# Reordering GpSimd's and SyncE's queues in a fused attention and mixture-of-experts kernel: the context's second sum, the result stores, the two real rows, and a third residual buffer

## The chip, the cores and the metric

The kernel runs on one core of a Trainium2 chip. The core has five engines, each with its own in-order instruction queue: TensorE (PE in the profile; its weight loads are PEld), VectorE (DVE), ScalarE (ACT), GpSimd (POOL) and SyncE (SP). SyncE and GpSimd issue the transfers of this kernel: SyncE plain ones, GpSimd those that add into their target and those with a list of rows ("indirect"). A queue that waits for a semaphore holds everything behind it.

The metric is the device time of one execution in microseconds (us). All data are 32-bit floats.

## What is computed

The reference is cut here to its steps:

```python
# attention, for 32 sequences of 512 tokens x 512 channels
q   = layernorm(x) * (1 + 0.1 * (s - 0.5)) * (1 + 0.1 * wave)   # s: ten logistic steps of sigmoid(|row|)
Q, K, V = q @ Wq.T + bq, mem @ Wk.T + bk, mem @ Wv.T + bv       # mem: the context times a constant
Qf, Kf, Vf = (fft(t, axis=sequence) for t in (Q, K, V))
QKV = hamilton(hamilton(Qf * filt, Kf * filt), Vf * filt)       # quaternion products of four channel blocks
x   = x + ifft(QKV).real
# mixture of experts over all 16384 tokens, 8 experts, a capacity for each
tokens = layernorm(x, gamma, beta)
logits = tokens @ gate_weight.T
top1, weight = argmax(logits), softmax(logits)[top1]            # weight is zero for tokens over the capacity
h   = gelu(dispatch @ wi[e]);  expert_out = h @ wo[e]           # 512 -> 2048 -> 512
out = x + weight * expert_out
```

A Fourier transform over 512 positions becomes matrix products with fixed tables. The spectrum of a real sequence is symmetric, so half of it is computed. Sums and differences of a sequence's front half and its mirrored rear half (the "folds") let the tables be half as large. Two lines of the spectrum are purely real (the first, and the middle one); they sit together in one partition and get a product of their own.

## The kernel before, in words

**Stages.** `attention_and_routing` handles the 32 sequences one after the other. I call each a *row*; b is its number. Then `experts` gathers the tokens of each expert, multiplies with its weights by a block scheme with fewer products (line 1226), and adds into the output by indirect stores (line 1378). A row's attention takes about one row period, but its work is spread over three: its context and x come in during the two rows before, and its normalisation, routing and stores happen in the rows behind.

**The order of the work** is written by hand. Every step is put into a heap with a due time, `at(time, function, ...)`, and `steps(...)` does it for a sequence of small ones. base[b] is the due time at which row b begins, 57.5 planner units after the row before. The heap is emptied in order of time, and `in_order` (line 158) then pins each engine's instructions to that order. So due times are only an order. What an engine really does when depends on the data.

**A row on TensorE**: the forward tables on the folded context (`ps_cf`, line 531) and on the folded query input (`ps_qf`, lines 539 and 544); then six projections k0, q0, v0, k1, q1, v1 (`pp_k`, `pp_q`, `pp_v`, line 576), which share two PSUM buffers in turn; between them the inverse tables of the row before (`back`, line 728), transposes and router logits of older rows. I give times inside a row from its first `ps_cf` matmul: "+25" is 25 us after it.

**The context's path.** `load_ctx` brings the direct half of the context by SP (line 454) and the mirrored half by two indirect loads of POOL (`behind`, line 273). POOL adds the halves (`add_ctx` 0, line 464), ScalarE negates the mirrored half (`minus_ctx`, line 459), and POOL adds the input once more from DRAM (`add_ctx` 1, line 464, `ctx<-in_ctx`), which gives the difference. VectorE folds both (`fold_ctx`, line 483, `cs<-ctx`) in the next row, ahead of the blocks of `pp_k` (line 595) that end the use of `pp_k`'s PSUM buffer.

**The two real lines' path** (`real_lanes`, from line 606). ScalarE copies them from the projections into a small tile `ny` (line 584) for k, q and v. SP stores it to DRAM (`nyid<-ny`, line 612) and loads it back spread over the partitions (`nyi<-nyid`, line 620). POOL multiplies in 15 small operations (lines 630 to 643). SP stores the product (`nyod<-nyo`, line 651) and puts it into `y` (`y<-nyod`, line 655), which the inverse tables (`back`) read.

**The residual's path.** ScalarE copies the sine part (`sines`, line 735), VectorE makes sum and difference (`part`, lines 742 and 745; `upper`, line 748), POOL adds the odd part (`lower`, line 755, `r<-y`) and then the input x (`add_input`: line 762 direct, line 273 twice indirect, `r<-in_x`). From r come the norms, the tokens (line 853), the result (line 861), and two stores (`store`, lines 865 to 872): the tokens by SP (`tokbuf<-tok`, line 869), and the result as a direct half by SP (`out<-r`, line 871) and two indirect stores by POOL (line 273, `out<-r,back`). The stores to `out` wait for one another, since all write the same tensor. The pool `resp` holds r in two buffers.

**POOL's queue in a row before**, from the middle of one row to the middle of the next: `r<-y`; `r<-in_x` and its two indirect parts; four scatters of routing entries (`meta<-entry,slot`, line 988); the product of the two real lines; the two indirect result stores; `ctx<-in_ctx` (the second sum); `qs<-x` and `x<-x` (line 496); the next context's indirect loads.

Due times that the change touches stand in one line each for the context (its fields are tx, tn, ta, tf, tl, cf, cl, cn, c0, c1) and for the real lines:

```python
}.get(b, (13.2, 17.4, 18.7, 31.0, 40.5, 16.3, 19.4, 44.4, 29.0, 53.0))
real_lanes(b, o + 35.1, *((o + 42.5, o + 48.3) if last else (o + 46.0, o + 58.5)))
at(o2 + 48.5, store, b, a["out"], "r")
```

Of the kernel before, what the change touches and what calls it, by code (L numbers as in the profile page):

```python
# [11 lines left out]
F32 = mybir.dt.float32  # L12
I32 = mybir.dt.int32
AF = mybir.ActivationFunctionType
ALU = mybir.AluOpType
# [203 lines left out]
def attention_and_routing(tc, a, gain, ident, gamma, beta, tokbuf, meta):  # L219
    nc = tc.nc  # L220
# [15 lines left out]
    with ExitStack() as es:  # L236
# [11 lines left out]
        yp = pool("yp", 1)  # L248
        resp = pool("resp", 2)
        tokp = pool("tokp", 1)  # L250
# [16 lines left out]

        def behind(b, ap, tiles, store=False, add=False):


            for h, t in enumerate(tiles):
                at_row = bass.IndirectOffsetOnAxis(ap=back[:, b, h : h + 1], axis=0)
                ins = nc.gpsimd.indirect_dma_start(
                    out=ap if store else t,
                    out_offset=at_row if store else None,
                    in_=t if store else ap,
                    in_offset=None if store else at_row,
                    bounds_check=n_tok - 1,
                    oob_is_err=False,
                    **({"compute_op": ALU.add} if add else {}),  # L280
                )
            return ins

# [167 lines left out]
        def load_ctx(b):  # L451

            w[b]["ctx"] = c = inp.tile([P, 2, H, D], F32, tag="ctx", name=f"ctx_{b}")
            nc.sync.dma_start(c[:, 0], onward(ctx_in[b]))
            behind(b, flat_rows(ctx_in), [c[:, 1, h] for h in range(H)])

# [103 lines left out]
        def project(b, n, c, t0, t1, t_blk):  # L560
# [20 lines left out]
            def real_rows():  # L581
                if "ny" not in w[b]:
                    w[b]["ny"] = nyp.tile([1, 3, 2, D], F32, tag="ny", name=f"ny_{b}", bufs=1)
                nc.scalar.copy(w[b]["ny"][:, i], w[b][key][0:1])

# [15 lines left out]
            if c == 0:  # L601
                at(done + 0.55, real_rows)
            at(t_blk, block, slice(0, 4, 3), ALU.subtract)
            at(t_blk + 0.6, block, slice(1, 3), ALU.add)

        def real_lanes(b, t, t_mul, t_out):

            def out():  # L610
                w[b]["nyid"] = dr.tile([6, D], F32, tag="nyid", name=f"nyid_{b}")
                nc.sync.dma_start(
                    w[b]["nyid"].rearrange("n d -> (n d)").unsqueeze(0),
                    w[b]["ny"].rearrange("o n l d -> o (n l d)"),
                )

            def back_in():
                w[b]["nyi"] = nyp.tile([P, 3, 2, 2, 2], F32, tag="nyi", name=f"nyi_{b}", bufs=1)
                with nc.allow_non_contiguous_dma(reason="two rows"):
                    nc.sync.dma_start(  # L620
                        w[b]["nyi"].rearrange("p n l h j -> p (n l) h j"),
                        w[b]["nyid"].rearrange("n (h f j) -> f n h j", h=2, j=2),
                    )
# [29 lines left out]
            def back():  # L653
                with nc.allow_non_contiguous_dma(reason="two rows"):
                    marks["row"] = nc.sync.dma_start(
                        w[b]["y"][0:1, 0].rearrange("o r (g f) -> o (r g) f", f=P),
                        w[b]["nyod"].rearrange("f x -> x f").unsqueeze(0),
                    )

            at(t, out)  # L660
            at(t + 3.8, back_in)
            steps(t_mul, 0.1, multiply())
# [94 lines left out]
        def add_input(b, way):  # L757
            r = w[b]["r"]
            if way:
                behind(b, flat_rows(x_in), [r[:, 2 * h + 1] for h in range(H)], add=True)  # L760
            else:
                nc.gpsimd.dma_start(r[:, 0::2, :], onward(x_in[b]), accum_op=ALU.add)
# [35 lines left out]
        def residual(b, t0, t1, t_in):  # L798

            for c, t in enumerate((t0, t1)):  # L800
                at(t, inverse, b, c)
                at(t + 1.85, sines, b, c)
                at(t + 2.5, part, b, c, 0)
                at(t + 3.1, part, b, c, 1)
            at(t1 + 3.7, upper, b)
            at(t1 + 4.6, lower, b)
            for way in range(2):
                at(t_in + 0.5 * way, add_input, b, way)
# [55 lines left out]

        def store(b, to, n):

            rows = to[b * S : (b + 1) * S, :]
            if n == "tok":
                marks[n, b] = nc.sync.dma_start(tok_rows(rows), w[b][n])
            else:  # L870
                nc.sync.dma_start(onward(rows), w[b][n][:, 0::2, :])
                marks[n, b] = behind(b, to, [w[b][n][:, 2 * h + 1] for h in range(H)], store=True)

# [186 lines left out]
        for b in range(B):  # L1060
# [5 lines left out]
                1: (27.8, 30.9, 32.0, 40.0, 50.0, 27.5, 30.5, 49.2, 40.0, 53.0),  # L1066
            }.get(b, (13.2, 17.4, 18.7, 31.0, 40.5, 16.3, 19.4, 44.4, 29.0, 53.0))
            if b + 1 < B:
# [28 lines left out]
            if b == 0:  # L1097
                real_lanes(b, o + 45.4, o + 53.0, o + 60.0)
                pt = 29.2, 51.2, 60.2, 38.2, 61.6, 71.0
            else:  # L1100
                real_lanes(b, o + 35.1, *((o + 42.5, o + 48.3) if last else (o + 46.0, o + 58.5)))
                if last:
                    pt = 30.6, 40.4, 49.2, 53.0, 62.4, 71.2
                else:
                    pt = 30.6, 41.6, 51.0, 54.4, 64.2, 73.6
# [15 lines left out]
            if b < B - 2:  # L1121
# [3 lines left out]
                steps(o2 + 12.5, 0.42, norms(b))  # L1125
                at(o2 + 30.0, store, b, tokbuf, "tok")
                at(o2 + 48.5, store, b, a["out"], "r")
                for dc, (t0, t1) in enumerate(((33.35, 35.5), (37.25, 38.3), (44.6, 45.2), (52.95, 53.6))):
                    at(o2 + t0, transposes, b, dc, range(TC))
                    at(o2 + t1, turned, b, dc)  # L1130
                lp, sh, lg, ch, cd, ct, rk, we, pl, sc = (
                    (66.25, 70.05, 73.15, 74.0, 0.5, 83.0, 85.65, 89.0, 90.0, 102.5)
                    if b < B - 3
# [11 lines left out]
            elif b == B - 2:  # L1145
                for t in range(TC):
                    at(end + 15.2 + 0.72 * t, token, b, t)
                    at(end + 34.0 + 0.72 * t, result, b, t)
                steps(end + 12.5, 0.17, norms(b))
                at(end + 17.9, store, b, tokbuf, "tok")  # L1150
                at(end + 37.0, store, b, a["out"], "r")
                for dc in range(DC):
# [12 lines left out]
            else:  # L1165
# [4 lines left out]
                for t in range(TC):  # L1170
                    at(end + 28.2 + 0.72 * t, token, b, t)
                    at(end + 40.7 + 0.72 * t, result, b, t)
                    for dc in range(DC):
                        at(end + 31.5 + 0.72 * t, transposes, b, dc, (t,), lambda dc=dc: two(dc))
                at(end + 31.1, store, b, tokbuf, "tok")
                at(end + 43.6, store, b, a["out"], "r")
                for dc in range(DC):
# [74 lines left out]
def experts(tc, a, ident, gamma, beta, tokbuf, meta, marks):  # L1252
# [9 lines left out]
    with ExitStack() as es:  # L1262
# [41 lines left out]

        with after(marks["row"]):
            wi = [load_wi(0, g) for g in range(G)]
        for g, t in enumerate(wi):
# [79 lines left out]

        with after(marks["r", B - 2]):
            wo = load_wo(0)
        xt = turn(0, 0, gather(0, 0))  # L1390
# [74 lines left out]
```

## Time and profile before

| what | value |
|---|---|
| median of 3 runs | 3630.23 us (3629.61 to 3639.62) |
| the profiled execution | 3633.5 us, its span 3631.8 us |
| mean granted TensorE clock | 0.983 |
| busy PE, DVE, ACT, POOL | 3484.9, 2465.1, 1513.3, 1197.4 us |
| row 0's first matmul to the last projection of row 31 | 13.6 to about 1939.9 us |
| from there to the first expert's first transpose (`ept`) | 1939.9 to 2027.5 us |
| experts, to the end of the span | 2036.5 to 3631.8 us |

The profile shows one execution. Busy times are sums of instruction lengths; they do not say which engine others waited for. That stands in the waits: "PE pp_v L576 <- DVE before L943" means that TensorE stood before a projection and that VectorE's instruction of line 943 was the last thing to end before it went on. The instruction named is the last in VectorE's order, so the true cause may lie some instructions earlier on VectorE. In a timeline each row is an instruction or a run of equal ones: its start from the span's start, its length, engine, line, what it writes and reads, and in brackets how long its engine sat idle before it and what ended that. "L464 POOL DMA_DIRECT2D" is the issue of a transfer by GpSimd; the transfer lands later.

### The profile page before, as it was taken

Reading aid. Unit: us, or ns where it says so; the run is one execution under the profiler, and the core shown is the slowest. Engines: PE = TensorE matmul, PEld = TensorE weight load, DVE = VectorE, ACT = ScalarE, POOL = GpSimd, SP = SyncE. Lnnn points to the kernel's source line nnn. Section 1 sums busy time; section 2 is a strip of 40 time slices with the busy share of each in tenths; the row PEclk is TensorE's granted clock in tenths of the full one; section 3 lists DMA queues with packets and bytes.
Section 4 is the critical chain, followed back from the end, with each engine's and each line's share of the span. In section 5 each row is a group of like instructions: output and inputs, shape, how many; then the busy total and the mean of one; then the engine's idle time right before and its main releaser. Section 6 shows DMA issues by size and latency. Waiting matters only on the chain. (4 is left out here: it accounts for less than half of the span.)

```text
span 3631.8 us, 39890 instructions
## 1 busy us (share of the span) xinstructions
PE 3484.9 (96%) x14080; PEld 2419.9 (67%) x14080; DVE 2465.1 (68%) x4430; ACT 1513.3 (42%) x2885; POOL 1197.4 (33%) x1166
## 2 busy tenths in 40 slices
PE   8899999999999999999996699999999999999998
PEld 4454555455555555555553588888888888888887
DVE  7998889798989898988887544353444444443532
ACT  5676677667555555555553211211212222211111
POOL 2344545455555454646553211110011111111100
PEclk9999999999999999999997899999999999999999
DMA  6767777676666667575736212130313121111200
GB/s 206 173 162 170 176 168 182 164 185 152 151 142 138 152 131 159 124 168 117 169 76 158 61 47 70 36 101 13 104 32 105 35 87 41 53 58 42 87 1 1
DMA packets 313064, 399.27 MB, mean 110 GB/s; under 512 B 115072, under 2 KB 181120, under 8 KB 312832
## 3 DMA queue, kind: packets, MB, share of 16 engines
q0 software_dynamic: 81040, 189.44, 26.0%
q1 hardware_dynamic: 230096, 207.01, 18.9%
q8 instruction: 111, 1.82, 0.2%
q14 instruction: 89, 0.73, 0.1%
q10 hardware_dynamic: 1728, 0.27, 0.0%
HBM read 239.37 MB, written 85.00 MB: 89 GB/s over the span
## 5 line engine op out<-in xcount | busy, mean ns | idle before, releaser
L1226 PE MATMUL r_o<-wo,h 128*128 128x256 f32 x3584 | 781.2, 379 | 0.0
L1226 PE MATMUL r<-xt,wi 128*128 128x256 f32 x3584 | 778.7, 380 | 0.8 <-DVE u L1241 0.8
L1226 PEld LDWEIGHTS r<-xt,wi 128*128 128x128 f32 x3584 | 682.2, 190 | 93.9 <-DVE u L1241 1.1
L1226 PEld LDWEIGHTS r_o<-wo,h 128*128 128x128 f32 x3584 | 677.5, 190 | 90.3
L576 PE MATMUL pp_v<-wv,cf 128*128 128x512 f32 x1024 | 472.5, 605 | 43.9 <-DVE before L943 37.6
L576 PE MATMUL pp_q<-wq,qf 128*128 128x512 f32 x1024 | 457.3, 595 | 0.9 <-DVE blk L595 0.9
L576 PE MATMUL pp_k<-wk,cf 128*128 128x512 f32 x1024 | 458.0, 595 | 0.0
L1378 POOL DMA_INDIRECT out<-o,ids x64 | 106.9, 1671 | 912.1 <-ACT o L1375 802.9
L576 PEld LDWEIGHTS pp_v<-wv,cf 128*128 128x128 f32 x1024 | 194.7, 194 | 288.6 <-issue 233.5
L1404 ACT ACTIVATE h<-h 128x512 f32<-128x512 f32 x256 | 160.0, 629 | 474.0 <-DVE h L1234 473.7
L576 PEld LDWEIGHTS pp_k<-wk,cf 128*128 128x128 f32 x1024 | 187.3, 190 | 225.2 <-issue 220.2
L576 PEld LDWEIGHTS pp_q<-wq,qf 128*128 128x128 f32 x1024 | 189.8, 190 | 217.4 <-issue 216.3
L1339 POOL DMA_INDIRECT g<-tokbuf,ids x64 | 80.6, 1259 | 509.9 <-PE ept L1357 491.7
L1375 ACT ACTIVATE o<-u_o,wgt 128x256 f32<-128x256 f32 x96 | 43.5, 500 | 385.4 <-DVE u_o L1234 385.4
L988 POOL DMA_INDIRECT meta<-entry,slot x128 | 175.0, 1367 | 57.7 <-issue 38.4
L1234 DVE TENSOR_TENSOR h<-r,u 128x512 f32<-128x512 f32 x192 | 129.6, 686 | 73.3 <-PE r L1226 73.1
L1241 DVE TENSOR_TENSOR u_o<-r_o,p_o 128x512 f32<-128x512 f32 x16 | 11.1, 691 | 239.7 <-PE r_o L1226 239.7
L892 ACT ACTIVATE tokT<-pt,beta,gamma 128x512 f32<-128x512 f32 x124 | 95.8, 774 | 156.1 <-PE pt L881 155.4
L699 DVE TENSOR_TENSOR pa<-pa,pb 128x1024 f32<-128x1024 f32 x128 | 157.4, 1230 | 2.9
L701 DVE TENSOR_TENSOR pa<-pa,pb 128x1024 f32<-128x1024 f32 x128 | 156.0, 1219 | 0.0
L696 DVE TENSOR_TENSOR pb<-blk 128x1024 f32<-128x1024 f32 x128 | 155.9, 1218 | 0.0
L696 DVE TENSOR_TENSOR pa<-blk 128x1024 f32<-128x1024 f32 x128 | 155.8, 1217 | 0.1
(212 smaller groups left out, 5376.6 us busy)
## 6 DMA issues: line engine op xcount, KB each, us to landing
xs<-in_x SPq DMA_DIRECT2D x32, 1024.0 KB, 6.8
x<-in_x SPq DMA_DIRECT2D x32, 1024.0 KB, 7.2
tokbuf<-tok SPq DMA_DIRECT2D x32, 1024.0 KB, 13.3
wi<-in_wi SPq DMA_DIRECT2D x64, 512.0 KB, 3.9
wo<-in_wo SPq DMA_DIRECT2D x32, 1024.0 KB, 5.1
qs<-x POOLq DMA_DIRECT2D x61, 512.0 KB, 5.1
ctx<-in_ctx SPq DMA_DIRECT2D x32, 512.0 KB, 3.8
r<-in_x POOLq DMA_DIRECT2D x32, 512.0 KB, 8.4
```

Of the source, the lines that this page charges most:

```text
L576: nc.tensor.matmul(w[b][key][:, ri, :], w[b][f][:, dc, lo : lo + P], wt[n][:, dc, :], start=(dc == 0), stop=(dc == DC - 1),)
L696: tt(out, _bc(left, full), right, ALU.mult)
L699: tt(pa[:, :, 0], pa[:, :, 0], pb[:, :, 1], ALU.subtract)
L701: tt(pa[:, :, 1], pa[:, :, 1], pb[:, :, 0], ALU.add)
L892: nc.scalar.activation(to, ps, AF.Identity, bias=o, scale=g)
L988: nc.gpsimd.indirect_dma_start(out=meta[t], out_offset=bass.IndirectOffsetOnAxis(ap=w[b]["slot"][:, t : t + 1], axis=0), in_=entry[:, b, t ...
L1226: nc.tensor.matmul(to[:, m, :], lhs(a, m, i), rhs(b, i), start=(i == 0), stop=(i == k - 1))
L1234: tt(c[i], x, y, ALU.add)
L1339: nc.gpsimd.indirect_dma_start(out=t, out_offset=None, in_=tokbuf, in_offset=bass.IndirectOffsetOnAxis(ap=gid[:, e, c : c + 1], axis=0), b ...
L1375: nc.scalar.activation(o[:, d * N : (d + 1) * N], c[2 * h + d][:, m, :], AF.Copy, scale=wgt[:, e, col : col + 1])
L1378: nc.gpsimd.indirect_dma_start(out=a["out"], out_offset=bass.IndirectOffsetOnAxis(ap=tid[:, e, col : col + 1], axis=0), in_=o, in_offset=None,
L1404: [lambda o=o: nc.scalar.activation(o, o, AF.Gelu) for o in out],
```

## The change

- **The context's second sum** is due at 44.5 rather than 53.0, and the negation ahead of it at 41.5 rather than 44.4 (rows 2 on; rows 0 and 1 keep theirs). On POOL it then stands behind `r<-in_x` and ahead of the product of the two real lines.
- **The product** stands ahead of the four scatters.
- **The result store** is split into `store_on` (SP, direct half) and `store_behind` for h = 0 and 1 (POOL, indirect). In rows up to 28 the order is: h = 0 ahead of `r<-in_x`, h = 1 after the scatters, and the direct half in the next row, behind `y<-nyod` on SP. The last three rows keep the direct half first.
- **nyid** is stored in three pieces of 4 KB, one after each of the copies for k, q and v, through a one-buffer tile of 4 KB; before it was one store of 12 KB after the last copy.
- **The odd part** (lines 745 and 748) is due 1.6 later; on VectorE one of the matrix product's operations (1.22 us) goes ahead of it.
- **`resp`** has three buffers. The buffer is 8 KB per partition; `ny` shrinks by as much.
- **Row 30's results** are due ahead of row 31's tokens on ScalarE.
- **Expert 0's weights**: three quarters of wi are loaded after row 30's `y<-nyod`, the last quarter and wo after row 31's; before, all of wi came after row 31's and wo after row 30's result store.

TensorE's order is unchanged. The diff's core:

```diff
-        resp = pool("resp", 2)
+        resp = pool("resp", 3)
...
             def real_rows():
-                if "ny" not in w[b]:
-                    w[b]["ny"] = nyp.tile([1, 3, 2, D], F32, tag="ny", name=f"ny_{b}", bufs=1)
-                nc.scalar.copy(w[b]["ny"][:, i], w[b][key][0:1])
+                w[b]["ny", n] = nyp.tile([1, 2, D], F32, tag="ny", name=f"ny_{n}_{b}", bufs=1)
+                nc.scalar.copy(w[b]["ny", n], w[b][key][0:1])
+
+            def real_rows_out():
+                if "nyid" not in w[b]:
+                    w[b]["nyid"] = dr.tile([3, 2 * D], F32, tag="nyid", name=f"nyid_{b}")
+                nc.sync.dma_start(w[b]["nyid"][i : i + 1], w[b]["ny", n].rearrange("o l d -> o (l d)"))
...
                 at(done + 0.55, real_rows)
+                at(done + 1.65, real_rows_out)
...
-            at(t, out)
-            at(t + 3.8, back_in)
+            at(t, back_in)
...
-                at(t + 2.5, part, b, c, 0)
-                at(t + 3.1, part, b, c, 1)
-            at(t1 + 3.7, upper, b)
-            at(t1 + 4.6, lower, b)
+                at(t + 2.5 + 1.6 * c, part, b, c, 0)
+                at(t + 3.1 + 1.6 * c, part, b, c, 1)
+            at(t1 + 5.3, upper, b)
+            at(t1 + 6.2, lower, b)
...
-            else:
-                nc.sync.dma_start(onward(rows), w[b][n][:, 0::2, :])
-                marks[n, b] = behind(b, to, [w[b][n][:, 2 * h + 1] for h in range(H)], store=True)
+        def store_on(b):
+            nc.sync.dma_start(onward(a["out"][b * S : (b + 1) * S, :]), w[b]["r"][:, 0::2, :])
+
+        def store_behind(b, h):
+            marks["r", b] = behind(b, a["out"], h, w[b]["r"][:, 2 * h + 1], store=True)
...
-            }.get(b, (13.2, 17.4, 18.7, 31.0, 40.5, 16.3, 19.4, 44.4, 29.0, 53.0))
+            }.get(b, (13.2, 17.4, 18.7, 31.0, 40.5, 16.3, 19.4, 41.5, 29.0, 44.5))
...
-                real_lanes(b, o + 35.1, *((o + 42.5, o + 48.3) if last else (o + 46.0, o + 58.5)))
+                real_lanes(b, o + 38.9, *((o + 39.5, o + 48.3) if last else (o + 45.0, o + 58.5)))
...
-                at(o2 + 48.5, store, b, a["out"], "r")
+                if b < B - 3:
+                    at(o2 + 40.2, store_behind, b, 0)
+                    at(o2 + 52.0, store_behind, b, 1)
+                    at(o2 + 65.0, store_on, b)
+                else:
+                    at(o2 + 42.9, store_on, b)
+                    at(o2 + 44.5, store_behind, b, 0)
+                    at(o2 + 51.0, store_behind, b, 1)
...
-                    (66.25, 70.05, 73.15, 74.0, 0.5, 83.0, 85.65, 89.0, 90.0, 102.5)
+                    (66.25, 70.05, 73.15, 74.0, 0.5, 83.0, 85.65, 89.0, 90.0, 104.5)
...
-                    at(end + 34.0 + 0.72 * t, result, b, t)
+                    at(end + 25.4 + 0.7 * t, result, b, t)
...
-                at(end + 37.0, store, b, a["out"], "r")
+                at(end + 28.3, store_on, b)
+                for h in range(H):
+                    at(end + 28.3 + (0.1, 1.7)[h], store_behind, b, h)
...
-        with after(marks["row"]):
-            wi = [load_wi(0, g) for g in range(G)]
+        with after(marks["row", B - 2]):
+            wi = [load_wi(0, g) for g in range(G - 1)]
+        with after(marks["row", B - 1]):
+            wi.append(load_wi(0, G - 1))
+            wo = load_wo(0)
...
-        with after(marks["r", B - 2]):
-            wo = load_wo(0)
```

More of the change, by code (lines that the diff above doesn't have):

```diff
@@ L266, in onward, with behind @@
             return ap.rearrange("(h w p) d -> w p h d", h=H, p=P)[0]
[L268 to L282, printed above, removed]
+        def behind(b, ap, h, t, store=False, add=False):
+            at_row = bass.IndirectOffsetOnAxis(ap=back[:, b, h : h + 1], axis=0)
+            return nc.gpsimd.indirect_dma_start(
+                out=ap if store else t,
+                out_offset=at_row if store else None,
+                in_=t if store else ap,
+                in_offset=None if store else at_row,
+                bounds_check=n_tok - 1,
+                oob_is_err=False,
+                **({"compute_op": ALU.add} if add else {}),
+            )
         w = [{} for _ in range(B)]
@@ L454, in load_ctx @@
             nc.sync.dma_start(c[:, 0], onward(ctx_in[b]))
-            behind(b, flat_rows(ctx_in), [c[:, 1, h] for h in range(H)])
+            for h in range(H):
+                behind(b, flat_rows(ctx_in), h, c[:, 1, h])
         def minus_ctx(b):
@@ L606, in real_lanes @@
         def real_lanes(b, t, t_mul, t_out):
[L610 to L615, printed above, removed]
             def back_in():
@@ L621, in back_in @@
                         w[b]["nyi"].rearrange("p n l h j -> p (n l) h j"),
-                        w[b]["nyid"].rearrange("n (h f j) -> f n h j", h=2, j=2),
+                        w[b]["nyid"].rearrange("n (l h f j) -> f (n l) h j", l=2, h=2, j=2),
                     )
@@ L654, in back @@
                 with nc.allow_non_contiguous_dma(reason="two rows"):
-                    marks["row"] = nc.sync.dma_start(
+                    marks["row", b] = nc.sync.dma_start(
                         w[b]["y"][0:1, 0].rearrange("o r (g f) -> o (r g) f", f=P),
@@ L759, in add_input @@
             if way:
-                behind(b, flat_rows(x_in), [r[:, 2 * h + 1] for h in range(H)], add=True)
+                for h in range(H):
+                    behind(b, flat_rows(x_in), h, r[:, 2 * h + 1], add=True)
             else:
@@ L863, in result, with store_tokens @@
             )
[L865 to L869, printed above, removed]
-            else:
-                nc.sync.dma_start(onward(rows), w[b][n][:, 0::2, :])
-                marks[n, b] = behind(b, to, [w[b][n][:, 2 * h + 1] for h in range(H)], store=True)
+        def store_tokens(b):
+            marks["tok", b] = nc.sync.dma_start(tok_rows(tokbuf[b * S : (b + 1) * S, :]), w[b]["tok"])
+        def store_on(b):
+            nc.sync.dma_start(onward(a["out"][b * S : (b + 1) * S, :]), w[b]["r"][:, 0::2, :])
+        def store_behind(b, h):
+            marks["r", b] = behind(b, a["out"], h, w[b]["r"][:, 2 * h + 1], store=True)
         def transposes(b, dc, ts, psum=None):
@@ L1097, in attention_and_routing @@
             if b == 0:
-                real_lanes(b, o + 45.4, o + 53.0, o + 60.0)
+                real_lanes(b, o + 49.0, o + 53.0, o + 60.0)
                 pt = 29.2, 51.2, 60.2, 38.2, 61.6, 71.0
             else:
-                real_lanes(b, o + 35.1, *((o + 42.5, o + 48.3) if last else (o + 46.0, o + 58.5)))
+                real_lanes(b, o + 38.9, *((o + 39.5, o + 48.3) if last else (o + 45.0, o + 58.5)))
                 if last:
@@ L1125, in attention_and_routing @@
                 steps(o2 + 12.5, 0.42, norms(b))
-                at(o2 + 30.0, store, b, tokbuf, "tok")
-                at(o2 + 48.5, store, b, a["out"], "r")
+                at(o2 + 30.0, store_tokens, b)
+                if b < B - 3:
[6 more added lines that the diff above has]
+                    at(o2 + 51.0, store_behind, b, 1)
                 for dc, (t0, t1) in enumerate(((33.35, 35.5), (37.25, 38.3), (44.6, 45.2), (52.95, 53.6))):
@@ L1147, in attention_and_routing @@
                     at(end + 15.2 + 0.72 * t, token, b, t)
-                    at(end + 34.0 + 0.72 * t, result, b, t)
+                    at(end + 25.4 + 0.7 * t, result, b, t)
                 steps(end + 12.5, 0.17, norms(b))
-                at(end + 17.9, store, b, tokbuf, "tok")
-                at(end + 37.0, store, b, a["out"], "r")
+                at(end + 17.9, store_tokens, b)
+                at(end + 28.3, store_on, b)
+                for h in range(H):
+                    at(end + 28.3 + (0.1, 1.7)[h], store_behind, b, h)
                 for dc in range(DC):
@@ L1174, in attention_and_routing @@
                         at(end + 31.5 + 0.72 * t, transposes, b, dc, (t,), lambda dc=dc: two(dc))
-                at(end + 31.1, store, b, tokbuf, "tok")
-                at(end + 43.6, store, b, a["out"], "r")
+                at(end + 31.1, store_tokens, b)
+                at(end + 43.6, store_on, b)
+                for h in range(H):
+                    at(end + 43.6 + (0.1, 1.7)[h], store_behind, b, h)
                 for dc in range(DC):
```

## The prediction

> **What bounds the kernel now.** I read the busy times first, then what TensorE waited for, then single rows in order of time. The profiled execution took 3633.5 us (span 3631.8); the runs' median is 3630.23, so its own time is 3.3 above the median. Busy times (us, share of the span, count):
> ```profile
> PE 3484.9 (96%) x14080; PEld 2419.9 (67%) x14080; DVE 2465.1 (68%) x4430; ACT 1513.3 (42%) x2885; POOL 1197.4 (33%) x1166
> ```
> TensorE's waits (total us, times, longest):
> ```profile
> PE pp_v L576 <- DVE before L943: 37.6, 17, 5.7
> ...
> PE lg L911 <- ACT tokT L905: 14.1, 3, 12.2
> ...
> PE back L728 <- DMA y<-nyod: 10.5, 2, 6.7
> ```
> TensorE is the bound, so a change that leaves its work alone can only win its gaps. The page's 96% hides two places. The experts' 1595 us (from 2036.5) are matmul without gaps and stay. In the 32 rows of attention, row 3 starts at 197.5 and row 31 at 1881.5: 1684 us for 28 rows. Rows without a gap take 58.27 (the start of row 15 to that of row 16 is 58.3), 28 of them 1631.6; the excess is **52.4 us**, 40 of it in rows 3 to 14. (It is more than the waits' sum because after a wait of 4.6 us or more the next four to eight matmuls come every 0.86 us instead of 0.43.) Two rows by windows (columns: length, then busy us of PE, PEld, DVE, ACT, POOL, granted clock, DMA share, GB/s):
> ```profile
> 379.70:445.40 65.70, 60.02 (x209) 32.40 (x208) 52.83 (x92) 43.34 (x92) 36.16 (x37) 0.97 0.78 192
> 937.00:995.30 58.30, 58.30 (x210) 31.86 (x209) 53.49 (x99) 32.59 (x58) 29.68 (x29) 1.00 0.65 145
> ```
> What the slow row waited for stands in its timeline (start, length, engine, line, operation; in brackets the idle time before it and its releaser):
> ```profile
> 394.27 1.81 POOL L273 DMA_INDIRECT out<-r,back  x1 [0.16 <-issue]
> 399.34 0.98 POOL L273 DMA_INDIRECT out<-r,back  x1 [3.27 <-ACT qs L491]
> 400.32 1.37 POOL L464 DMA_DIRECT2D ctx<-in_ctx  x1
> 406.46 1.23 DVE L483 TENSOR_TENSOR cs<-ctx 128x1024 f32<-128x1024 f32 x1 [8.03 <-PE back L728]
> 410.50 0.68 DVE L595 TENSOR_TENSOR blk<-pp_k,xz_k 128x512 f32<-128x512 f32 x1
> 412.03 1.19 PE L576 MATMUL pp_v<-wv,cf 128*128 128x512 f32 x1 [5.68 <-DVE before L943]
> ```
> POOL issues the context's second sum behind the real rows' products and both strided stores. It lands about 6 us later; VectorE, whose order is fixed, stands 8.03 us before the fold that reads it, and the blocks that free pp_k's PSUM buffer stand behind the fold. The releasers printed are the last ones by the profile (back had long been done); the transfer is the true one. Over all rows the fold's idle time is 90.5 us:
> ```profile
> L483 DVE TENSOR_TENSOR cs<-ctx 128x1024 f32<-128x1024 f32 x62 | 75.6, 1221 | 90.5 <-issue 44.9 <-DMA ctx<-in_ctx 23.0 <-PE back L728 15.8
> ```
> Row by row the landing after the row's start (first number) gives the row's length (second): 4: 25.3, 65.7; 5: 19.7, 58.2; 6: 26.6, 65.7; 7: 22.4, 60.0; 11: 25.9, 65.6; 13: 21.9, 59.6; 14: 25.9, 64.9; 15: 19.0, 58.3. The fold is ready for its data at +17.7 to +18; some 2 us of lateness are free.
>
> The second place is the end of row 31:
> ```profile
> 1940.08 0.69 SPq L655 DMA_DIRECT2D y<-nyod  x1
> 1946.61 3.75 PE L728 MATMUL back<-y,inv 128*128 128x512 f32 x4 [6.71 <-DMA y<-nyod]
> 1953.75 0.97 POOL L273 DMA_INDIRECT out<-r,back  x1 [6.14 <-issue]
> 1959.71 0.59 ACT L735 COPY r<-back 128x512 f32<-128x512 f32 x1 [19.15 <-DMA out<-r,back]
> 1960.33 1.29 DVE L742 TENSOR_TENSOR r<-back,r 128x512 f32<-128x512 f32 x2 [13.05 <-ACT r L735]
> ```
> ScalarE waits 19.15 us for the buffer of row 29's result, VectorE 13.05 behind it, and the chain goes on serially to the first expert's matmul at 2027.5.
>
> **The change part by part.** *Context's sum (due 53.0 to 44.5), negation (44.4 to 41.5).* On POOL it now goes right behind the three issues of r<-in_x, which are done at +50 to +56 of the row before (they wait for r<-y, landing +49 to +51 in rows 3 to 14, +43 to +45 later). Issue 1.4, landing 5.9: it is there by about +4 of its row, 14 us ahead of the fold. The negation it needs ends at +45 to +53 today and moves earlier. Rows with landing under 20 show what remains: nothing. Upper bound: all 52.4. Lower: half the early rows' 40.2 and all of the later rows' 12.2, 32. I take **45**, nearest to rows 5 and 15, leaving 7 for waits with other causes (VectorE is busy 52.8 to 53.5 of 58.3, so small lateness stays).
>
> *What is queued behind it.* The multiply (15 small operations, 8.5 to 10.6 us) starts 1.4 later by the sum but ahead of four scatters (1.367 each, 5.5) and the stores: it ends at about +6 of the next row; nyod and y<-nyod (6.3 to 9.3 to landing) are in by +18, needed by back at +24.7. Free. The scatters are read only after row 31. qs<-x waits for ScalarE at +19.9 as now: free, if the second strided store leaves by then. It is issued at +8 to +15.5 and no longer waits 3.27 for the first one's landing, which lies 15 us back.
>
> *Result stores in three.* Same bytes. The direct half, last in the write order, waits on SP for the second strided half: +13 to +20 (landing 4.1 after issue). Behind it on SP stand nyid for k, the context's load and the following xs. The context's load left at +25.7 (471.35 in the row of 445.4), so it has 5 us.
>
> *nyid in three 4 KB stores, one 4 KB buffer.* SP issues 64 more DMAs of 0.25 to 0.4 us, on an idle queue. ScalarE's copy for q (at +25.5) must now find k's store landed: issued at +18.7 (copy at +17.6, 1.0 long) to +20.8, landing 1.4 (nyod, 4 KB) to 7 later (nyid's 12 KB to nyi's issue in busy rows; 1.5 to 3 in quiet ones). So +20.1 to +27.8: 0 to 2.3 us of ScalarE's time in busy rows, where pp_q's buffer is needed only some 5 us later. I take 0; at 2.3 in rows 3 to 14 and no cover it is 28. In return nyi waits for 4 KB rather than 12: 0 to 3 us sooner, off the chain except in row 1, whose y<-nyod wait is 3.98. I take **2** for rows 1 and 2 (0 to 6); row 2's 3.9 stands behind VectorE's exponential (ex_e, L211) and stays.
>
> The rule that speaks against this: the Trainium skill, "DMA: Bandwidth & Descriptors", section Bandwidth, calls transfers under 64 KB descriptor-dominated and says to batch; its section on the gpsimd path gives about 2.0 us fixed for each DMA. By that, as an estimate, 64 more are 128 us if all were exposed. The trace has 1.4 us for nyod's 4 KB; the sum counts by where these lie, and two of three lie off the chain.
>
> *VectorE's odd part moved 1.6 later:* one product (1.22 us, L696) goes ahead of a wait (L745 for y of ScalarE, 92.4 us over 32 rows). It fills idle time; r<-y then leaves up to 0.7 to 1.2 later. Between −1 and +1 per row; 0.
>
> *Third residual buffer, and the end.* Row 31's r no longer needs row 29's store. L735 then follows back_0. The multiply(31) goes ahead of r<-in_x(30): from 1929.4 to nyi's landing at 1924.4, 5 us, so y<-nyod lands about 1941 and L742 runs at 1946 to 1947 instead of 1960.3: −13 to −14. Next late are r<-in_x(30), now issued at about 1934 to 1939 and landing 8 later, 1947 (for L815, at 1961.7 today), and row 31's own stores and scatters on POOL. Bounds: −8 (the sum into r at 1952) to −18 (the 19.15 but for one matmul group). I take **−13**.
> *Weights of expert 0 in two marks, results of row 30 ahead of tokens(31):* loads of 3.9 to 5.1 us with 70 us to spare, and ScalarE idles there: 0.
>
> Sum: 45 + 2 + 13 = 60; 3633.5 − 60 = 3573.5 in a profiled execution, against the median 3630.2 − 60 = **3570**.
>
> **Rivals.** (A) *Early rows keep their stall*: in rows 3 to 14 (DMA share 0.72 against 0.63) SP's new wait delays k's store and the context's load. The gain is 12.2, 13 and a quarter of 40.2: 35, giving 3595. For it: 0 to 2.3 us by the bounds above; against: 5 us of cover. (B) *VectorE becomes the bound*: rows settle near 59.0, 0.7 × 28 = 20 lost: 3590. For it: only 4.8 us free in a row of 58.3; against: row 15 keeps 58.3. (C) *The sum was not the cause*: VectorE's backlog would be; only the end gains: 3617. Against: the row table. (D) *Slower*: the single nyid buffer stops ScalarE each row, since SP holds k's store until the second strided store has landed. It decides from where the rows lose over 60/29 = 2.1 us each, i.e. ScalarE held some 7 us (5 of cover), k's store landing at about +32.5, 5 past my bound. At 4 us a row: 29 × 4 − 60 = +56, 3686. For it: a chain POOL–SP–ScalarE that was not there; against: the bounds.
>
> **How the numbers follow.** Forecast 0.54, A 0.17, B 0.10, C 0.07, D 0.12. 0.3% (11 us) is about what a measurement tells from no change. A, B and the forecast are faster, of C (13 us against 11) about half, and a sliver of A's bad side falls within: 0.83 faster, 0.05 same, 0.12 slower. The likeliest's own range is 3554 (52.4 + 6 + 18 = 76 off) to 3590; A, B and the small end (32 + 0 + 8 = 40 off: 3590) with A's bad side (rows −10, end −8: 3612) and C reach 3618; D alone is left out.
>
> **What would show it.** Right: the fold's idle time of 90.5 falls below 20; the wait of pp_v from 37.6 to under 8; rows of 58.3 from 3 on; L735's 19.15 gone; row 31 starts some 47 us earlier. (A) shows as copies of ny waiting on nyid, (D) likewise in every row, (B) as rows of 59 without waits on transfers. The prediction is wrong if k's store leaves SP after +25, or if L815 waits for r<-in_x until after 1955.

## The result

The changed kernel took 3576.18 us in the median of four runs (3565.53 to 3581.87), against 3631.66 for the kernel before. The ratio is 0.984, with a 95% interval of 0.9812 to 0.9868: 55 us faster. I had forecast 3570, with a range of 3554 to 3618. The profiled execution has a span of 3576.6 us.

Where the 55.2 us between the two profiled spans lie, measured between the same instructions in both traces:

| stretch | before | changed | difference | forecast |
|---|---|---|---|---|
| rows 0 to 2 (first matmul to the start of row 3) | 184.0 | 185.0 | +1.1 | −2 |
| rows 3 to 30 (start of row 3 to start of row 31) | 1684.0 | 1643.3 | −40.7 | −45 |
| end (last projection of row 31 to the first `ept`) | 87.6 | 74.3 | −13.3 | −13 |
| all else | 1676.3 | 1674.0 | −2.3 | 0 |

The same lines as before, from the changed kernel's waits of TensorE (total us, times, longest) and its groups:

```profile
PE ept L1369 <- DMA g<-tokbuf,ids: 23.4, 4, 20.6
...
PE back L724 <- DMA y<-nyod: 9.9, 2, 5.3
PE back L724 <- DVE y L715: 6.5, 1, 6.5
...
PE back L724 <- ACT r L731: 5.5, 2, 2.9
PE pp_v L575 <- DVE ex_e L211: 4.5, 1, 4.5
PE lg L909 <- ACT tokT L903: 4.4, 3, 2.6
```
```profile
L482 DVE TENSOR_TENSOR cs<-ctx 128x1024 f32<-128x1024 f32 x62 | 75.4, 1218 | 0.0
L582 ACT COPY ny_q<-pp_q 1x1024 f32<-1x1024 f32 x32 | 31.8, 993 | 13.2 <-DMA nyid<-ny_k 13.2
L731 ACT COPY r<-back 128x512 f32<-128x512 f32 x32 | 18.7, 583 | 13.2 <-PE back L724 11.8
```

The old main wait, `pp_v` behind VectorE's line 943 with 37.6 us, is gone from the list. The fold of the context (`cs<-ctx`) has lost all of its 90.5 us of idle time. The copy of the sine part no longer waits for `out<-r,back`, and the wait of `lg` at the end has gone from 14.1 to 4.4.

Two waits are new. `back` waits for ScalarE in two rows, and ScalarE's copy for q (`ny_q`) waits 13.2 us for k's store of `nyid`. 26 of the 28 rows take 58.3 us; row 7 takes 65.3 and row 11 takes 62.8. Row 7 in order of time, SyncE's queue and then ScalarE's and TensorE's part:

```profile
455.61 0.39 SPq L867 DMA_DIRECT2D out<-r  x1
456.09 1.08 SPq L587 DMA_DIRECT2D nyid<-ny_k  x1
457.35 0.39 SPq L452 DMA_DIRECT2D ctx<-in_ctx  x1
...
464.82 0.24 SPq L587 DMA_DIRECT2D nyid<-ny_q  x1
```
```profile
463.80 1.00 ACT L582 COPY ny_q<-pp_q 1x1024 f32<-1x1024 f32 x1 [6.59 <-DMA nyid<-ny_k]
464.70 0.57 ACT L731 COPY r<-back 128x512 f32<-128x512 f32 x1
```

The direct result store `out<-r` stands ahead of k's store on SyncE. In this row it left 24.0 us after the row's start (it waited for the second strided store of GpSimd), k's store left at +24.5, and it had landed at +32.2. The copy for q was due at +25.5. ScalarE's copy of the sine part came 6.5 us late, and TensorE, which needs its PSUM buffers back, waited 2.9 us and then ran at half pace. The window of the row (length, busy PE, PEld, DVE, ACT, POOL, granted clock, DMA share, GB/s):

```profile
431.59:496.93 65.34, 61.62 (x209) 32.84 (x208) 53.90 (x112) 43.12 (x92) 39.11 (x42) 0.95 0.71 169
```

Rows 7 and 11 were hit because GpSimd's product took longer there: 15.4 and 15.1 us, against 9.9 to 12.9 in the other rows from 4 to 14. It began no later (3.3 us ahead of the row's start, as in rows 4, 10 and 13), but its first operation took 5.4 us, against 0.7 to 2.0 in the others. Row 6 and row 7 (starts of rows: 373.32 and 431.59), the product's first operation and the issue of `qs<-x` that follows the second strided store:

```profile
371.16 1.33 POOL L640 TENSOR_TENSOR nyi<-nyi,bias 128x12 f32<-128x12 f32 x1
393.22 0.96 POOL L495 DMA_DIRECT2D qs<-x  x1 [2.93 <-ACT qs L490]
...
428.29 5.40 POOL L640 TENSOR_TENSOR nyi<-nyi,bias 128x12 f32<-128x12 f32 x1
453.56 1.01 POOL L495 DMA_DIRECT2D qs<-x  x1
```

In the kernel before this operation took 0.2 to 1.1 us in rows 4 to 15. Why it is longer behind the sum's issue, and 5.4 us in these two rows, no run shows.

At the end, VectorE's sum into r starts 9.0 us after the last projection (at 1900.2 here) rather than 20.4 (1960.33 against 1939.9):

```profile
1897.09 0.69 SPq L652 DMA_DIRECT2D y<-nyod  x1
...
1904.84 3.75 PE L724 MATMUL back<-y,inv 128*128 128x512 f32 x4 [4.62 <-DMA y<-nyod]
...
1908.63 0.58 ACT L731 COPY r<-back 128x512 f32<-128x512 f32 x1 [7.74 <-PE back L724]
1909.24 1.29 DVE L738 TENSOR_TENSOR r<-back,r 128x512 f32<-128x512 f32 x2 [2.76 <-ACT r L731]
```

### The profile page after: what moved, and what is told of

Same layout as the page of the kernel before. It is cut to its first block, busy times and chain, and to the rows that moved or that the text cites. A ratio compares the mean times of both kernels' runs of the same rounds, so it can differ in the third digit from the quotient of the medians.

```text
span 3576.6 us, 39943 instructions
## 1 busy us (share of the span) xinstructions
PE 3477.1 (97%) x14080; PEld 2424.8 (68%) x14080; DVE 2468.7 (69%) x4430; ACT 1511.7 (42%) x2885; POOL 1185.0 (33%) x1166
## 3 DMA queue, kind: packets, MB, share of 16 engines
q1 hardware_dynamic: 230224, 207.01, 18.7%
## 5 line engine op out<-in xcount | busy, mean ns | idle before, releaser
L575 PE MATMUL pp_v<-wv,cf 128*128 128x512 f32 x1024 | 464.3, 597 | 4.5 <-DVE ex_e L211 4.5
L986 POOL DMA_INDIRECT meta<-entry,slot x128 | 185.0, 1445 | 57.6 <-issue 31.8
```

Source lines behind the costliest of these rows:

```text
L575: nc.tensor.matmul(w[b][key][:, ri, :], w[b][f][:, dc, lo : lo + P], wt[n][:, dc, :], start=(dc == 0), stop=(dc == DC - 1),)
L986: nc.gpsimd.indirect_dma_start(out=meta[t], out_offset=bass.IndirectOffsetOnAxis(ap=w[b]["slot"][:, t : t + 1], axis=0), in_=entry[:, b, t ...
```

## The experiments

Four questions were open. Is the stall of rows 7 and 11 k's store on SyncE, and does it make the changed kernel's times spread? Is the rows' gain the sum's place alone? What is each part of the end's 13 us worth? Which parts of the change are needed? Because the times of the kernel before also differ between chips (medians of 3631.7 to 3641.4), ratios to it are given. Each profile's *row loss* below is the length of rows 3 to 30 less 28 × 58.27 = 1631.6 us; its *end* runs from the last projection of row 31 to the first `ept`. In the kernel before these are 52.4 and 87.6, in the changed one 11.7 and 74.3. Row loss and end are read from one profiled execution of each kernel, so they need not add up to the difference of the medians.

### The stall in rows 7 and 11

**The changed kernel again.**

> The changed kernel unaltered, to see how far its own executions lie apart. My theory: rows 7 and 11 of the profiled execution lost 7.0 and 4.5 us because ScalarE's copy for q waited until k's 4 KB store had landed; which of the busy rows 3 to 14 are hit, and how many, differs from execution to execution, so the times spread from about 3565 (no row hit) to 3582. The rival, that the spread is noise of the whole program as in the kernel before (3629.6 to 3639.6), expects the same spread, but also in the next two kernels.

Five runs gave 3571.36 in the median, and 3567.45, 3570.45, 3571.36, 3582.74 and 3586.82 in all; ratio 0.9836 (0.9813 to 0.9859). In its profile only row 7 is long (60.0), the row loss is 1.8, and the copy for q waits 7.7 us over three rows, 5, 6 and 7. So the rows that are hit do differ from one execution to the next. That the two slowest runs had more of them is not shown, since they left no trace; the next two kernels speak for it.

**The direct store behind k's store and the context's load.**

```diff
-                    at(o2 + 65.0, store_on, b)
+                    at(o2 + 77.2, store_on, b)
```

> Only the due time of the direct half of the result store is moved in rows up to 28 (65.0 to 77.2), so that on SP it stands behind k's nyid store and the context's load instead of ahead of them. Theory: k's store then never waits for the second strided result store, leaves at +18.7 in every row and lands by +25; no row is hit, the median falls by 8 to 12 us to about 3565, and the executions lie within some 4 us of each other. Rival (k's store is late because the transfer engines are full, not because of its place on SP): copies for q still wait, the median stays at 3574 to 3578.

Median 3566.49, runs from 3565.66 to 3568.10, ratio 0.9807 (0.9794 to 0.9821). Row 7's part of SyncE's queue is now

```profile
449.62 0.25 SPq L587 DMA_DIRECT2D nyid<-ny_k  x1
452.24 0.38 SPq L452 DMA_DIRECT2D ctx<-in_ctx  x1
452.73 1.27 SPq L867 DMA_DIRECT2D out<-r  x1
457.47 0.24 SPq L587 DMA_DIRECT2D nyid<-ny_q  x1
```

k's store leaves at +18.7 in every row from 3 on, no copy for q waits, and the row loss is 0.1. The spread fell from 19.4 us to 2.4. The rival is not without ground: transfers of GpSimd slow the store that stands ahead of k's, as the last section shows.

**Two buffers for `ny`.**

```diff
-                w[b]["ny", n] = nyp.tile([1, 2, D], F32, tag="ny", name=f"ny_{n}_{b}", bufs=1)
+                w[b]["ny", n] = nyp.tile([1, 2, D], F32, tag="ny", name=f"ny_{n}_{b}", bufs=2)
```

> Only the tile ny gets two buffers of 4 KB instead of one; SP's order stays. Theory: the copy for q then waits for v's store of the row before, which landed 30 us earlier; ScalarE isn't held and the median falls to about 3565 too, though k's store is as late as before. Rival (what is late in rows 7 and 11 is POOL's queue itself, and the wait on ny is only the last to end): another wait takes its place and the median stays above 3573.

Median 3567.93 (3566.30 to 3570.82), ratio 0.9812 (0.9798 to 0.9826), row loss 0.2. In its profile k's store left as late as +23.8 (row 10), and nobody waited for it. So the link that costs is the one between k's landing and the copy for q. Either end of it can be cut: an earlier store, or a second buffer.

### The rows' gain

**The sum alone, on the kernel before.**

```diff
-            }.get(b, (13.2, 17.4, 18.7, 31.0, 40.5, 16.3, 19.4, 44.4, 29.0, 53.0))
+            }.get(b, (13.2, 17.4, 18.7, 31.0, 40.5, 16.3, 19.4, 41.5, 29.0, 44.5))
```

> The kernel before with the two due times alone (sum 53.0 to 44.5, negation 44.4 to 41.5): the sum stands behind r<-in_x and ahead of the scatters and the product, nothing else differs. Theory: the rows' gain is the sum's alone; the wait of pp_v behind VectorE (37.6 us) falls under 8, rows 3 to 30 give 42 to 52 us, the end gives nothing: 3578 to 3590. Rival 1 (the gain needs the stores taken apart as well, since they hold POOL): half of it, 3600 to 3612. Rival 2 (VectorE's own backlog): 3625 to 3635.

Median 3597.23 (3594.19 to 3598.75), ratio 0.9879 (0.9859 to 0.9899), in microseconds between the theory and rival 1, though 44.2 below the median of the kernel before on the same chip. The fold has no idle time left, so the cause of the old stall was the sum's late issue. But the row loss is still 17.9. The waits of TensorE and the fold's group:

```profile
PE back L728 <- DMA y<-nyod: 19.9, 8, 7.1
PE lg L911 <- ACT tokT L905: 14.0, 3, 12.1
```
```profile
L483 DVE TENSOR_TENSOR cs<-ctx 128x1024 f32<-128x1024 f32 x62 | 75.5, 1218 | 0.0
```

The wait of `back` for `y<-nyod` rose from 10.5 us in 2 waits to 19.9 in 8. The product of the two real lines now stands behind the sum and the scatters on GpSimd, and `y<-nyod` leaves at +15.8 to +20.8 in rows 4 to 14 (+9.4 to +15.9 before). One wait took the place of another. (In row 25, a quiet one, it leaves only 0.7 us later, at +11.6; why it is more in the early rows was not taken apart.)

**The sum, and the product ahead of the scatters.**

```diff
-            }.get(b, (13.2, 17.4, 18.7, 31.0, 40.5, 16.3, 19.4, 44.4, 29.0, 53.0))
+            }.get(b, (13.2, 17.4, 18.7, 31.0, 40.5, 16.3, 19.4, 41.5, 29.0, 44.5))
...
-                real_lanes(b, o + 35.1, *((o + 42.5, o + 48.3) if last else (o + 46.0, o + 58.5)))
+                real_lanes(b, o + 35.1, *((o + 42.5, o + 48.3) if last else (o + 45.0, o + 58.5)))
...
-                    (66.25, 70.05, 73.15, 74.0, 0.5, 83.0, 85.65, 89.0, 90.0, 102.5)
+                    (66.25, 70.05, 73.15, 74.0, 0.5, 83.0, 85.65, 89.0, 90.0, 104.5)
```

> The kernel before with the sum's and the negation's new due times and with the product of the two real lines ahead of the scatters (46.0 to 45.0, 102.5 to 104.5); result stores, nyid, buffers and odd part stay as before. The sum alone left 17.9 us in the rows, with y<-nyod late at back (19.9 us in 8 waits). Theory: the product starts 5.5 us earlier, those waits go, the rows keep under 5 us, the end stays as before: 3580 to 3588; the stores need not be taken apart. Rival (POOL still holds qs<-x behind both stores until +22 to +26, and that stalls the rows in turn): 3592 or above.

Median 3578.55 (3577.62 to 3579.90), ratio 0.9842 (0.9826 to 0.9859). Every row from 3 to 30 takes 58.3, the row loss is 0.1, and the end is as long as before (87.8):

```profile
PE ept L1357 <- issue: 21.3, 1, 21.3
PE lg L911 <- ACT tokT L905: 13.5, 3, 11.7
PE ps_cf L531 <- DMA xs<-in_x: 13.5, 1, 13.5
PE back L728 <- DMA y<-nyod: 7.4, 1, 7.4
```

`qs<-x` leaves as late as +23.1 in the busy rows, as the rival said, and nothing in the rows waits for it. These due times alone bring as much as the whole change did in its own comparison.

**The changed kernel with the sum back.**

```diff
-            }.get(b, (13.2, 17.4, 18.7, 31.0, 40.5, 16.3, 19.4, 41.5, 29.0, 44.5))
+            }.get(b, (13.2, 17.4, 18.7, 31.0, 40.5, 16.3, 19.4, 44.4, 29.0, 53.0))
```

> The changed kernel with the sum and the negation at their due times of before: on POOL the sum stands behind product, scatters and the second strided store, but no longer behind the wait for the first one's landing (3.3 us) and its issue. Theory (the sum's place decides): it lands at about +23 in rows 3 to 14 and +17 later, so that the busy rows keep a stall of 2 to 4 us each and the later ones none: 3595 to 3615. Rival (the stores taken apart give the gain, the sum's place nothing): 3570 to 3582.

Median 3576.61 (3571.31 to 3579.22), ratio 0.9823 (0.9801 to 0.9845). My expectation missed by 20 to 40 us. The row loss is 9.4. The fold does wait again,

```profile
L482 DVE TENSOR_TENSOR cs<-ctx 128x1024 f32<-128x1024 f32 x62 | 75.6, 1221 | 28.6 <-issue 10.8 <-DMA ctx<-in_ctx 9.8 <-PE pp_q L575 8.1
```

but 28.6 us in place of 90.5, and only part of that reaches TensorE, since a row has some 2 us to spare. I had put the sum's issue at about +17 in the busy rows; it left at +10.5 to +16.7 in rows 4 to 14 but for row 11 (+19.6). Row 11 takes 64.6, with 2.0 us of waiting of the copy for q in it, rows 4 and 6 take 59.0 and 60.1, and the later rows 58.3. The first strided store, with its issue and the 3.3 us of waiting behind it, is no longer ahead of the sum. So there are two ways to most of the gain. The sum is early enough either when it is moved ahead of the product and the stores, or, nearly, when half of the stores is taken out of its way. (The product is ahead of the scatters in both kernels.)

### The end, and the parts left

**The third buffer, with the split `nyid` that makes room for it, on the kernel before.**

```diff
-        resp = pool("resp", 2)
+        resp = pool("resp", 3)
...
+                at(done + 1.65, real_rows_out)
...
-            at(t, out)
```

(`real_rows` and `real_rows_out` as in the change.)

> The kernel before with the third residual buffer, and nyid in three stores through the 4 KB tile (without which the third buffer has no room); sum, result stores, odd part and row 31's product stay as before. Theory: ScalarE's wait of 19.15 us for row 29's store goes, L735 follows back_0 at once and the end is 8 to 13 us shorter; the rows keep their stalls; 3617 to 3624. The split alone costs nothing, since SP has nothing ahead of k's store here. Rival (the single ny buffer costs time by itself, each row waiting for a landing): ScalarE waits behind nyid's stores in the busy rows and the time is 3630 or above.

Median 3622.01 (3616.94 to 3623.88), ratio 0.9945 (0.9924 to 0.9966). The row loss is 53.0, as before; the end is 78.9, that is 8.7 shorter. No copy into `ny` waits. The split costs the rows nothing by itself. The medians of this chip lie 19.4 us apart, twice what the two profiles show (9.6); the runs of the kernel before spread over 12.8 us there, and where the rest comes from is open.

**The changed kernel with two buffers.**

```diff
-        resp = pool("resp", 3)
+        resp = pool("resp", 2)
```

> The changed kernel with two residual buffers instead of three. I had counted the third buffer for row 31 alone. Theory now: with the direct half of the store held back to the next row it is needed in every row, since that half leaves at +18 to +24 in rows 4 to 14 and +11 to +13.5 later, lands about 8 us after, and row b+2's first sine copy wants the buffer at +25.5: a wait of 1 to 6 us in most of rows 4 to 14, none later, and 3 to 6 at the end: 3600 to 3635. Rival (the third buffer serves row 31 alone): 3574 to 3584.

Median 3579.56 (3574.95 to 3581.35), ratio 0.9842 (0.9825 to 0.9859). My theory fell, and the rival, which was the prediction's own view, holds. The copy of the sine part waits for a store once, at the end:

```profile
L731 ACT COPY r<-back 128x512 f32<-128x512 f32 x32 | 18.6, 583 | 22.3 <-DMA out<-r,back 17.0 <-PE back L724 4.0
```

The end is 83.3. The direct stores left at +17.4 to +22.7 in rows 4 to 14, and the copies, which waited for no store, went 6.2 to 9.5 us after them (at +26.6 in six of the eleven rows; in the other five ScalarE had been held by the copy for q). So the buffers were free by then.

**Row 31's product late.**

```diff
-                real_lanes(b, o + 38.9, *((o + 39.5, o + 48.3) if last else (o + 45.0, o + 58.5)))
+                real_lanes(b, o + 38.9, *((o + 42.5, o + 48.3) if last else (o + 45.0, o + 58.5)))
```

> The changed kernel with row 31's product of the two real lines behind r<-in_x of row 30 on POOL, as before. Theory: I counted this as 5 of the 13 us at the end; y<-nyod of row 31 leaves 5 us later and the first gather 4 to 6 us later: 3579 to 3583 against 3574 to 3578. Rival (the next-in-line r<-in_x of row 30, which now leaves 10 us later than it could, binds the end anyway): no difference or 1 to 3 us faster.

Median 3576.66 (3575.39 to 3577.72), ratio 0.9824 (0.9804 to 0.9843): by time, not to be told from the changed kernel. Its profile tells more: the end is 77.9, where the profiles of the kernels with the early product and three buffers show 74.3 to 77.0, and `y<-nyod` keeps `back` waiting 8.8 us there rather than 4.6 to 7.0. That is 1 to 4 us, less than the 5 I had counted.

**The odd part back.**

```diff
-                at(t + 2.5 + 1.6 * c, part, b, c, 0)
-                at(t + 3.1 + 1.6 * c, part, b, c, 1)
-            at(t1 + 5.3, upper, b)
-            at(t1 + 6.2, lower, b)
+                at(t + 2.5, part, b, c, 0)
+                at(t + 3.1, part, b, c, 1)
+            at(t1 + 3.7, upper, b)
+            at(t1 + 4.6, lower, b)
```

> The odd part (two differences and the half that uses them on VectorE, and the add of r<-y on POOL) gets its due times of before; all else as changed. I counted this part of the change at nothing. Theory: VectorE's idle time ahead of the odd part's first instruction, 57.9 us in the changed kernel and 92.4 before, goes back to 85 to 95, and the time stays within 5 us of the changed kernel since VectorE has slack once the context's sum is early (3571 to 3581). Rival: VectorE's slack of 5 us a row is what the rows of 58.27 live on, and 1.2 us less of it costs 0.5 to 1 us in each of 28 rows: 3590 to 3604.

Median 3568.62 (3566.73 to 3575.39), ratio 0.9812 (0.9799 to 0.9826). VectorE's idle time ahead of the odd part is 93.9 us, and apart from rows 7 and 12 (59.0 and 63.7), where the copy for q waits 6.7 us in all, the rows keep 58.3 or 58.4. This part of the change is worth nothing that can be measured.

**Three parts together: sum, product first, third buffer.** The edits of the kernels with sum and product, and with the third buffer, on the kernel before.

> The kernel before with three parts of the change: the sum's place, the product ahead of the scatters, and the third residual buffer with the split nyid that makes room for it. The result stores stay together, the odd part and row 31's product as before. Theory: the two gains are independent; the rows lose nothing (as in the kernel with sum and product alone) and the end is 9 us shorter than there: 3566 to 3571, with executions within 4 us of each other, since SP has no waiting store ahead of k's nyid store. So the stores taken apart are not needed for the gain. Rival (the rows' freedom from waits depends on the result stores' place once the third buffer lets everything run earlier): 3575 or above, or a spread above 10 us.

Median 3569.90 (3568.64 to 3570.72), ratio 0.9807 (0.9794 to 0.9821). Row loss 0.1, end 78.1, spread 2.1. The result stores stay as they were in the kernel before. Row 30's results and expert 0's weights stay so too; no run has these two by themselves. The ratio is that of the changed kernel with its direct store later, so what this kernel leaves out of the change is not seen in the time.

**A faster version.** The direct store moved behind k's, and one more edit, to a wait that both kernels have (`ex_e`, line 211, row 2):

```diff
-                    at(o2 + 65.0, store_on, b)
+                    at(o2 + 77.2, store_on, b)
...
-        steps(base[2] + 2.0, 0.85, factors(4, 7))
+        steps(base[2] + 24.0, 0.7, factors(4, 7))
```

> The changed kernel with the direct store behind k's nyid store and the context's load, as in the kernel of 3566.5, and with the small VectorE operations for the query factors of rows 4 to 6 (62 of 0.17 us) moved from due time 2.0 to 24.0 of row 2. Theory: row 2's wait of 4.5 us of pp_v behind them and the half-speed matmuls after it go, 5 to 7 us: 3559 to 3562. Rival (VectorE is behind in row 2 for its ordinary work, and the named operation is only the last to end): 3565 to 3568.

Median 3564.17 (3562.09 to 3565.74), ratio 0.9803 (0.9787 to 0.9820): the lowest median here, though its interval does not part it from the 0.9807 of the two versions above. In its profile row 2 takes 58.3 instead of 62.4, and the wait of `pp_v` behind `ex_e` is gone. The profiled execution is 6.0 us shorter than that of the kernel of 3566.49, but the medians differ by 2.3: the profiled execution was the fastest of its five here and the slowest of its five there. Row 2 does what I expected of it; in the runs less than half shows.

## Why the prediction was right, and where a step was off

- *The stall's cause* (the second sum, issued behind the product and both strided stores) was right. The fold's idle time went from 90.5 to 0.0, with the sum alone too. The releaser printed for it, `back`, was not the cause, as I had read it. In the changed kernel the sum lands 7.9 to 12.0 us after its issue in rows 4 to 14, as far as the trace has it, rather than 5.9, and is early enough all the same.
- *45 us in the rows.* 40.7 in the profiled execution. That the size comes out near is in part luck: the fold's stall was worth all of the 52.4, my upper bound (row loss 0.1 with the sum and the product moved and nothing else waiting), and 11.7 were lost again to a wait that I had put at 0. Row 31 starts 39.7 us earlier, not 47. The 7 us that I left for small lateness and VectorE's fullness (rival B) do not exist: rows of the changed kernel with 52.8 to 55.4 us of VectorE's work keep 58.3.
- *"ScalarE's time in busy rows: I take 0"* is the step that failed. I had the second strided store at +8 to +15.5; it left at +15.2 to +20.1 in rows 4 to 14 but for rows 8 and 12 (+11.5 and +13.7), because the product, which I had put at 8.5 to 10.6 us, took 10.5 to 15.4 and ended at +8.0 to +12.1 in these rows, not at +6, and four scatters come behind it. So k's store left at up to +24.5 rather than +20.8, and landed 7.7 later there. My bound for the landing, 7 us, was too low by the trace of before itself: `nyi<-nyid` waited up to 11.0 us for the landing of the 12 KB (its line stands below). The cover that I put at about 5 us is about 2: in the two profiles of the changed kernel, waits of the copy of 0.4, 1.8 and 2.1 us cost their rows nothing, one of 3.9 cost 1.7, and those of 6.3 and 6.6 cost 4.5 and 7.0. Rival A had the mechanism, SyncE's new wait, but it cost time in two rows of twelve, not in most of them.
- *64 more small stores at no cost.* Right for two of the three in a row, and in the kernels where nothing waits ahead of them on SyncE, for all. The Trainium skill ("DMA: Bandwidth & Descriptors") calls transfers under 64 KB descriptor-dominated in its section Bandwidth. Its 2.0 us fixed for each DMA, from which my estimate of 128 us came, stand in the section on the GpSimd path ("Anatomy of one DMA"), while these stores leave by SyncE. Neither is seen in the time of the kernel with the split alone (row loss 53.0 against 52.4). What cost was one store's place in a queue.
- *Rows 0 to 2: −2.* They lost 1.1. The last piece of `nyid` in row 0 is 4 KB rather than 12, but it was issued at 66.98 instead of 64.23, and `nyi<-nyid`, which waits for it, left at 78.34 instead of 69.26. I had taken fewer bytes for an earlier landing. In the second profile the piece left at 63.95, and the product still began no sooner than before (78.62 against 78.11), so the split gains nothing there; the term was nothing rather than 2. (Two readings were off: row 1's wait, given as 3.98, is 3.8 in the trace, and the context's load of row 7, given as +25.7, left at +25.9.)
- *The end: −13.* −13.3. The third buffer is the larger part, 8.7 alone (87.6 to 78.9) and 9.7 with the rows mended (87.8 to 78.1). I had said 5 for the early product; by the profiles it is 1 to 4, since `y<-nyod` was issued 3.1 us before the last projection's end rather than 0.2 after it and then took 7.7 us.
- *Odd part 0*: right. *Result stores in three*: counted as neither gain nor loss; they are not needed for the gain (3569.90 without them) and bring the one new wait.

The wait of `nyi<-nyid` in the kernel before (us in total, times, longest):

```profile
SPq L620 <- DMA nyid<-ny: 113.7, 32, 11.0
```

Rivals C and D are out: the sum was the cause, and the single `ny` buffer holds ScalarE in three rows in each of the two profiles of the changed kernel (five with two residual buffers), not in all.

## What to carry to other kernels

When an in-order engine waits before a step, look past the printed releaser to the transfer that the step reads, and then to what stands ahead of that transfer's issue on its queue. When a waiting store is put onto another queue, list what stands behind it there, and bound its issue from the whole chain that leads to it: here the last of that chain came up to 4.6 us later than its bound, and a 4 KB store behind it cost 11.5 us in one execution. Cutting the link at either end (order, or one more buffer) made the times both lower and steadier. A spread between executions can point at such a link but is no sure sign: the runs with row 31's product late lie within 2.3 us, and its profile has rows 5 and 11 hit.

## What I had not expected of the hardware

- A 4 KB store issued 0.5 us behind a 512 KB store on the same queue landed 4.7 to 7.9 us later in the rows where the copy for q waited for it. The copy starts at its landing, so this is read from rows 5, 7 and 11 of the changed kernel (issued +21.3, +24.5, +24.0; copy at +26.0, +32.2, +31.9) and rows 5, 6 and 7 of its second profile (+21.7, +21.5, +22.4; +27.7, +27.4, +29.5). `nyod`'s 4 KB land in a median of 1.4 us. These rows are not typical. By the trace's packet records, the store's one packet began 4.2, 7.0 and 7.0 us after the issue in rows 5, 7 and 11, but 1.6 to 1.9 us after it in the six other rows of the changed kernel with the same two stores in the same order, and 0.7 to 1.0 us after it in the 19 rows in which nothing stood close ahead. (In the kernel with the split alone, where no result store stands ahead, it is up to 3.6 us.) What differs is GpSimd's `qs<-x` and `x<-x`, 512 KB each: in rows 5, 7 and 11 they had been issued before `out<-r`, in the six others at the same time or later. In row 7, while they moved some 190 KB per us, `out<-r` began with about 60 KB per us; in row 6, ahead of them, it had 200 to 300. So the store was late behind a large store that was itself slowed by other transfers.
- TensorE ran at half pace (a matmul every 0.86 us instead of 0.43) after waits of 2.6 and 2.9 us in rows 11 and 7 of the changed kernel too, for three matmuls and about seven; the granted clock is 0.50 from 466.0 to 472.8 and from 705.0 to 708.4. In the kernel before, in rows 3 to 30, I had seen this only from 4.6 us on (for three to six matmuls, not the four to eight that I wrote), and not after 2.4. But row 1 of the kernel before, which I had left out, has a clock of 0.50 from 77.1 to 80.5, after waits of 2.0 and 0.2 us within 1 us. So the length of one wait does not decide it, and I can give no bound that both traces keep.
